# Router scores on GpSimd in two halves of four experts, with the queries' layer norms between them

## The chip, the cores and the metric

One Trainium2 chip, one of its cores. A core has a matrix engine (PE, whose weight loads are listed apart as PEld), a vector engine (DVE), a scalar engine (ACT), GpSimd (POOL) and SyncE (SP), which here only issues transfers. Each engine works through its own queue in order; semaphores tie the queues together. The metric is device time in microseconds of one execution: the median of repeated runs.

## The reference

One block of a network over 64 sequences of 32 rows with 256 features, so 2048 tokens, in float32:

```python
x = x + cross_attention(layernorm(x), ctx_512)   # 16 heads of 64, 257 context rows of 128 features per sequence
x = x + self_attention(layernorm(x))             # 4 heads of 64, rotary positions, within a sequence of 32
x = x + experts(layernorm(x))                    # 8 experts, each token goes to 2
# in experts:
scores = einsum('bsd,nd->bsn', x, Wr) + br       # [tokens, 8]: the router's scores
w = softmax(scores); idx = top_k(scores + biases_N, 2)
val = w[idx] / sum(w[idx])
y = sum over the 2 experts of val * ((silu(x @ Wl1a) * (x @ Wl1b)) @ Wl2 + biases)
```

The change touches how `scores` is computed for most tokens, and nothing else of the result.

## The kernel before

**Tiles and stages.** The tokens lie in 16 tiles of 128 rows; a tile t holds four sequences b. The main loop runs over the 64 pairs (t, b). For each it does cross-attention: scores of the next sequence (`cross_probs`, L305: four matmuls `s`, for each the negated maximum `nmx` on DVE at L319, the exponential on ACT at L320, then for two at a time a reciprocal and the scaling `pr` on DVE at L325 and L327), the transposes `tp` of the present sequence's probabilities in two groups (L338), and the mix `pa` with the context (L348). Everything else of a tile is done in small steps between these: while tile T is in its four sequences, the steps of tile T-1 ("near") and T-2 ("far") and the queries of the next pair of tiles ("ahead") are called at places given by a table, `steps` (L932), one row per sequence for an even and an odd tile, six places a row.

**The steps of a tile** (`rest`, L557) are 13 pieces between `yield`s: the value products `pov` and the cross output (1 to 3, ending in the layer norm "s"), then self-attention: transposes, qkv, the rotary products on DVE (4 to 6), the transposes `trqk`, scores and softmax, output (7 to 10, ending in the layer norm "r" into `xr`), then `route` (L475, 11 to 13): transposes `trr` of `xr`; the router's two matmuls `pr` with eight columns, the top two experts, softmax weights; and last `pk`, a matmul that ranks the tokens of each expert, from which follow `slots`, and two indirect transfers (scatters) of `xr` into the buffer `routed` in main memory. `carry` (L553) hands the running counts to the next tile with one small POOL operation.

**Queries.** `cross_queries(c)` (L250) makes the queries for tiles 2c and 2c+1: two layer norms "q", transposes `trq`, then products over several pieces. Its first piece, the norms, is called at the end of the last sequence of an odd tile.

**A layer norm** (`normed`, L173) is statistics, aggregate and adding epsilon on DVE, a power on POOL for the reciprocal root (L183), then one DVE operation (L186) that waits for it.

**Order.** PE and SP keep the order in which the program calls them. On DVE, ACT and POOL a planner sets the order when the program is built, except for instructions passed to `keep_in_program_order`. At run time each queue is fixed and in order: whatever waits at its head holds all that stands behind it.

**Buffers** that matter: PSUM banks `a` (three, used in turn by nearly all products outside the scores), `s` (three), `t` (two). `xr` has two buffers, so the writing of `xr` for tile t waits until the scatters of tile t-2 have landed.

After the last tile come the experts: six "early" blocks of 128 token rows whose experts are surely full, counted from the tiles ranked so far when the last tile begins, then "late" blocks, run over weights loaded into three lanes. They take the time from about 585 us on.

Of the kernel before, what the change touches and what calls it, by code (L numbers as in the profile page):

```python
# [9 lines left out]
FP = mybir.dt.float32  # L10
# [40 lines left out]
def block_kernel(  # L51
# [13 lines left out]
    awo: bass.AP,  # L65
    abo: bass.AP,
    freq: bass.AP,
    wr_t: bass.AP,
    br: bass.AP,
    bias_n: bass.AP,  # L70
# [96 lines left out]
    xp = pool("xp", 3)  # L167
    tb = pool("tb", 1)

    def bank(shape, name):  # L170
        return ps.tile([P] + shape, FP, tag="a", name=name)

# [77 lines left out]
    def cross_queries(c):  # L250

        xqT = wk.tile([P, 2, 2 * P], FP, tag="xqT", name=f"xqT{c}")

        xns = [normed(2 * c + j, "q", pinned=(c == 1)) for j in range(2)]
        yield
        for j in range(2):
            transposed(xqT[:, :, j * P : (j + 1) * P], xns[j], 2, f"q{2 * c + j}")


        qh = wk.tile([P, XH // 2, 2 * P], FP, tag="qh", bufs=1, name=f"qh{c}")  # L260
        q = qp.tile([P, 8, XH, SEQ], FP, tag="q", name=f"q{c}")
        queries[c] = q

        def of_heads(i):
            pq = [bank([2, 8, SEQ], f"pq{c}_{i}_{par}") for par in range(2)]
            for mm in range(2):
                m = 2 * i + mm
                for par in range(2):
                    r = par * HD
                    nc.tensor.matmul(  # L270
                        pq[par][:, mm, :, :].rearrange("p b n -> p (b n)"),
                        xwk_sb[r : r + HD, m, :],
                        qh[r : r + HD, m, :],
                        start=True,
                        stop=True,
                    )
            for par in range(2):
                dst = q[:, :, 4 * i + par : 4 * i + par + 3 : 2, :]
                dst = dst.rearrange("p b h n -> p h b n")
                if par:  # L280
                    nc.scalar.copy(dst, pq[par])
                else:
                    nc.vector.tensor_copy(dst, pq[par])

        for i in range(4):
            yield
            pq = bank([2, 2 * P], f"pqh{c}_{i}")
            for mm in range(2):
                m = 2 * i + mm
                for k in range(2):  # L290
                    nc.tensor.matmul(  # L291
                        pq[:, mm, :],
                        xwq_sb[:, k, m * P : (m + 1) * P],
                        xqT[:, k, :],
                        start=(k == 0),
                        stop=(k == 1),
                    )
            nc.scalar.mul(qh[:, 2 * i : 2 * i + 2, :], pq, QK_SCALE)
            if i:
                yield  # L300
                of_heads(i - 1)
        yield
        of_heads(3)
# [171 lines left out]
    def route(t, xr):  # L475

        nc.gpsimd.tensor_copy(xr[:, RW - 1 : RW], token[:, t : t + 1])
        xT = wk.tile([P, 2, P], FP, tag="xrT", name=f"xrT{t}")
        transposed(xT, xr, 2, f"r{t}", t < NT - 2)
        yield  # L480
        pr = bank([NE], f"pr{t}")
        for k in range(2):
            nc.tensor.matmul(pr, xT[:, k, :], wr_sb[:, k, :], start=(k == 0), stop=(k == 1))
        sc = sm.tile([P, NE], FP, tag="rsc", name=f"rsc{t}")
        nc.vector.tensor_tensor(sc, pr, br_bc, ALU.add)
        sel = sm.tile([P, NE], FP, tag="rsel", name=f"rsel{t}")
        nc.vector.tensor_tensor(sel, sc, bn_bc, ALU.add)
        top = sm.tile([P, 8], FP, tag="rtop", name=f"rtop{t}")
        nc.vector.max(top, sel)
        idx = sm.tile([P, 8], U32, tag="ridx", name=f"ridx{t}")  # L490
        nc.vector.max_index(idx, top, sel)
        idf = sm.tile([P, 2, 1], FP, tag="ridf", name=f"ridf{t}")
        nc.vector.tensor_copy(idf[:, :, 0], idx[:, 0:2])

        two = sm.tile([P, 2, NE], FP, tag="rtwo", name=f"rtwo{t}")
# [36 lines left out]
        nc.vector.tensor_tensor(at[:, 0, :], pk, region[:, 0, :], ALU.add)  # L532
        nc.vector.tensor_tensor(two, two, at.to_broadcast([P, 2, NE]), ALU.mult)
        slot = sm.tile([P, 2], FP, tag="rslot", name=f"rslot{t}")
        nc.vector.tensor_reduce(slot, two, AX.X, ALU.add)
        slots = sm.tile([P, 2], U32, tag="rslots", name=f"rslots{t}")
        nc.vector.tensor_copy(slots, slot)
        for k in range(2):
            nc.gpsimd.indirect_dma_start(  # L539
                out=routed[:, :],  # L540
                out_offset=bass.IndirectOffsetOnAxis(ap=slots[:, k : k + 1], axis=0),
                in_=xr,
                in_offset=None,
            )
        if t >= NT - 2:

            nc.gpsimd.dma_start(out=out[t * P : (t + 1) * P, :], in_=xs[t])
        if t < NT - 1:
            seen[t] = sm.tile([P, NE], FP, tag="seen", name=f"seen{t}")
            nc.vector.tensor_tensor(seen[t], pk, both, ALU.add)  # L550
            carry(t)
# [308 lines left out]
    def rotary_tables():  # L860
# [69 lines left out]


    steps = (  # L932
        ("", "far", "ahead", "near", "far", ""),
        ("near", "far", "", "near", "far", ""),
        ("ahead", "far", "ahead", "near", "far", "ahead"),
        ("near", "", "ahead", "near", "", "far"),
        ("", "far", "ahead", "near", "far", ""),
        ("near", "far", "", "near", "far", ""),
        ("ahead", "far", "ahead", "near", "far", "ahead"),
        ("", "", "near", "near", "", "far"),  # L940
    )
    last_steps = steps[4:6] + (
        ("", "", "far", "near", "", "far"),
# [1 line left out]
    )  # L945
    kvs, probs = {0: context0}, {}
    seqs = [(t, b) for t in range(NT) for b in range(4)]
    work = {"near": last_rows(), "far": iter(()), "ahead": cross_queries(0)}
    next(work["ahead"])

    diag = [const.tile([P, AH, P], FP, name=f"diag{i}") for i in range(2)]
# [85 lines left out]
    for n, (t, b) in enumerate(seqs):  # L1037
# [22 lines left out]
        def step():  # L1060
            name = next(place)
            if name:
                next(work[name], None)
# [4 lines left out]
            scores = cross_probs(t1, b1, kvs[t1][0])  # L1068
        pr, pts = probs.pop((t, b)), []
        probs_transposed(t, b, 0, pr, pts)  # L1070
        step()
        next(scores, None)
        next(scores, None)
# [15 lines left out]
        if b == 3:  # L1089
            if t < NT - 1:  # L1090
                load_last(t)
            if t % 2:
                for _ in work["ahead"]:
                    pass
                if t + 3 < NT:
                    work["ahead"] = cross_queries((t + 3) // 2)
                    next(work["ahead"])
            for _ in work["far"]:
                pass
            work["far"] = work["near"]  # L1100
            work["near"] = rest(t, cT, lastT, u_ring[t % 3])

# [144 lines left out]
```

## Time and profile before

| | us |
|---|---|
| median of 3 runs | 801.22 (800.99 to 802.54) |
| the profiled execution, its own time | 802.53 |
| its span, first to last instruction | 800.8 |
| PE busy | 771.7 (96%) |
| DVE busy | 503.1 (63%) |
| ACT busy | 365.3 (46%) |
| POOL busy | 152.4 (19%) |
| mean granted clock of PE | 0.993 |

The span falls in two parts: the 16 tiles (to about 585 us), in which all engines work, and the expert blocks, in which PE works nearly alone. In a timeline line the first number is the start in us, the second the busy time, then engine, source line, operation, what it writes and reads, sizes, the count, and in brackets the idle time before it with what ended it. In a line of a group the numbers after the bar are total busy us, mean ns of one, and idle time before, with its causes. In a table of stretches the columns are the stretch, its length, the busy time of PE, PEld, DVE, ACT and POOL, the granted clock, the share of the transfer engines and GB/s.

### The profile page before, as it was taken

To read this page: it belongs to the slowest core of one execution; us is meant where nothing else is said; L and a number is where in the kernel's file an instruction comes from. 1 tells how busy PE (TensorE), PEld (TensorE's weight loads), DVE (VectorE), ACT (ScalarE), POOL (GpSimd) and SP (SyncE) were. 2 spreads that over 40 slices of the span, in tenths; PEclk is the share of its full clock that TensorE was granted. 3 is DMA by queue.
4 is the path that set the end of the run, shared out by engine and by line. 5 is a ranking of instruction groups with operands and counts; after the bars stand their busy time and mean duration, and the time that the engine had idled before them with its cause. 6 is when DMAs were issued, how large, how long until landed. Compare 5 with 4: busy or idle time off the path is not lost. (4 is left out here: it accounts for less than half of the span.)

```text
span 800.8 us, 15293 instructions
## 1 busy us (share of the span) xinstructions
PE 771.7 (96%) x5146; PEld 604.5 (75%) x5146; DVE 503.1 (63%) x2084; ACT 365.3 (46%) x1052; POOL 152.4 (19%) x214
## 2 busy tenths in 40 slices
PE   8899999999999999999999999999999899999994
PEld 7576677677767777777767777676678799999994
DVE  4657666766686676677677766768665633554442
ACT  3564555555465555546554555555434222212220
POOL 3001011120211111111111111121124412332332
PEclk9999999999999999999999999999999999999997
DMA  9440102021120202021110202020351396458432
GB/s 309 142 111 2 67 11 68 11 89 27 53 73 18 67 11 80 11 69 50 50 60 18 68 11 67 10 78 15 119 203 34 80 398 180 54 110 251 58 45 28
DMA packets 44258, 64.17 MB, mean 80 GB/s; under 512 B 19408, under 2 KB 35152, under 8 KB 42640
## 3 DMA queue, kind: packets, MB, share of 16 engines
q1 hardware_dynamic: 37648, 54.08, 20.8%
q0 software_dynamic: 6528, 9.06, 6.2%
q8 instruction: 43, 0.70, 0.4%
q14 instruction: 39, 0.32, 0.1%
HBM read 87.54 MB, written 13.16 MB: 126 GB/s over the span
## 5 line engine op out<-in xcount | busy, mean ns | idle before, releaser
L320 ACT ACTIVATE pr<-s,nmx 128x257 f32<-128x257 f32 x256 | 122.2, 481 | 111.8 <-DVE nmx L319 100.5
L319 DVE TENSOR_REDUCE nmx<-s 128x1 f32<-128x257 f32 x256 | 105.4, 420 | 71.0 <-PE s L315 70.4
L315 PE MATMUL s<-kv,q 128*128 128x257 f32 x512 | 143.1, 388 | 1.9 <-ACT pr L320 1.9
L348 PE MATMUL pa<-pt,kv 128*128 128x512 f32 x256 | 123.2, 604 | 5.0 <-ACT ov L372 4.9
L315 PEld LDWEIGHTS s<-kv,q 128*128 128x128 f32 x512 | 89.3, 193 | 16.7 <-ACT pr L320 3.2
L338 PEld LDWEIGHTS tp<-ident,pr 128*128 128x128 f32 x512 | 61.8, 144 | 30.6 <-issue 15.7
L338 PE MATMUL tp<-ident,pr 128*128 128x128 f32 x512 | 80.5, 279 | 1.6 <-DVE pr L327 1.6
L327 DVE TENSOR_SCALAR pr<-pr,inv 128x256 f32<-128x256 f32 x256 | 79.7, 353 | 3.4
L351 ACT COPY cT<-pa 128x512 f32<-128x512 f32 x64 | 37.5, 586 | 91.4 <-PE pa L348 91.4
L342 ACT COPY pt<-tp 128x512 f32<-128x512 f32 x128 | 75.6, 591 | 4.5 <-PE tp L338 3.5
L348 PEld LDWEIGHTS pa<-pt,kv 128*128 128x128 f32 x256 | 46.1, 190 | 39.4 <-issue 26.6
L752 POOL DMA_INDIRECT out_x<-y_late,to_late x28 | 43.5, 1555 | 104.0 <-DMA out_x<-y_late,to_late 39.0
L291 PE MATMUL pqh<-xqT,xwq_sb 128*128 128x256 f32 x256 | 60.8, 381 | 0.8 <-ACT xqT L198 0.8
L381 PE MATMUL po<-xwo_sb,ov 128*128 128x256 f32 x256 | 60.6, 379 | 0.0
L381 PEld LDWEIGHTS po<-xwo_sb,ov 128*128 128x128 f32 x256 | 48.6, 190 | 6.6
L291 PEld LDWEIGHTS pqh<-xqT,xwq_sb 128*128 128x128 f32 x256 | 47.3, 190 | 7.9 <-ACT xqT L198 1.5
L320 ACT ACTIVATION_READ_ACCUMULATOR pr<-s,nmx 128x1 f32 x256 | 52.1, 203 | 0.0
L325 DVE RECIPROCAL inv<-sums 128x2 f32<-128x2 f32 x128 | 20.8, 162 | 46.7 <-ACT pr L320 45.8
L728 ACT ACTIVATE sa_late<-pa_late,lane 128x128 f32<-128x128 f32 x72 | 20.6, 369 | 63.6 <-PE pa_late L712 63.6
L555 POOL TENSOR_SCALAR carried<-seen,is_last 128x8 f32<-128x8 f32 x15 | 5.3, 353 | 218.6 <-DVE seen L550 218.6
L539 POOL DMA_INDIRECT routed<-xr,rslots x32 | 33.0, 1032 | 59.2 <-DMA routed<-xr,rslots 22.0
L396 PE MATMUL pqkv<-awqkv_sb,xaT 128*128 128x512 f32 (+1 forms) x128 | 43.9, 486 | 0.0
(275 smaller groups left out, 1270.8 us busy)
## 6 DMA issues: line engine op xcount, KB each, us to landing
lane<-in_wall SPq DMA_DIRECT2D x24, 1028.0 KB
lane<-in_wall SPq DMA_DIRECT2D x24, 640.0 KB
lane2a<-in_wall SPq DMA_DIRECT2D x10, 1028.0 KB
kv<-in_ctx_t SPq DMA_DIRECT2D x16, 514.0 KB
kv<-in_ctx_a SPq DMA_DIRECT2D x16, 512.0 KB
lane2b<-in_wall SPq DMA_DIRECT2D x10, 640.0 KB
xg_late<-routed SPq DMA_DIRECT2D x80, 32.0 KB
x<-in_x SPq DMA_DIRECT2D x16, 128.0 KB
```

The source lines that it names most:

```text
L291: nc.tensor.matmul(pq[:, mm, :], xwq_sb[:, k, m * P : (m + 1) * P], xqT[:, k, :], start=(k == 0), stop=(k == 1),)
L315: nc.tensor.matmul(s, qb[:, g * P : (g + 1) * P], kvT[:, b, :], start=True, stop=True)
L319: nc.vector.tensor_reduce(nmx, s, AX.X, ALU.max, negate=True)
L320: nc.scalar.activation(pr[:, g, :], s, AF.Exp, bias=nmx, accum_out=sums[:, g : g + 1])
L327: nc.vector.tensor_scalar(pr[:, i, :ML], pr[:, i, :ML], inv[:, i : i + 1], None, ALU.mult)
L338: nc.tensor.transpose(tp[:, g * P : (g + 1) * P], pr[:, g, j * P : (j + 1) * P], ident)
L342: nc.scalar.copy(pt, tp)
L348: nc.tensor.matmul(pa, kvA[:, b, j, :], pts[j], start=(j == 0), stop=(j == MC - 1))
L351: nc.scalar.copy(cT[:, :, b, :], pa.rearrange("p (h n) -> p h n", n=SEQ))
L381: nc.tensor.matmul(po, ov[:, m, :], xwo_sb[:, m, :], start=False, stop=(m == XH // 2 - 1))
L396: nc.tensor.matmul(pq, xaT[:, k, :], awqkv_sb[:, k, lo:hi], start=(k == 0), stop=(k == 1))
L752: nc.gpsimd.indirect_dma_start(out=out[:, :], out_offset=bass.IndirectOffsetOnAxis(ap=self.to[:, b : b + 1], axis=0), in_=y, in_offset=Non ...
```

## The change

For the tiles 0 to 12 the router's scores are computed without PE. POOL multiplies `xr` with each expert's weight row, spread over all 128 partitions, and folds the products by pairs of experts from 256 columns to 32; DVE then sums the 32 that are left, for all eight experts at once. The eight weight rows are loaded at the start into buffers that the expert blocks use later. The POOL work of a tile is in two steps, experts 0 to 3 and 4 to 7, a sequence apart in the table. Tiles 13 to 15 keep the old way, with the tile tag `xaT` for the transposed rows.

The steps of a tile are now 14, and a third stage, "late", holds a tile's last two: they are called in the first sequence of the tile after, at its first and last place, where the sum, the top two and the weights, and then `pk` and the scatters are made. `pk` thus moves from the end of a tile's fourth sequence to the end of the next tile's first one. The norms of the next queries are called at the start of an odd tile's fourth sequence instead of its end, ahead of the second half, and their first statistics are kept in program order, as are the multiplications and the sum.

```diff
+    wr_rows = []
+    for e in range(NE):
+        tag, bufs = (("y", 4), ("bxT", 2), ("wr_row", 2))[(e > 3) + (e > 5)]
+        wr_rows.append(xp.tile([P, D], FP, tag=tag, bufs=bufs, name=f"wr_row{e}"))
+        load(wr_rows[e], wr[e, :].partition_broadcast(P))
...
-        xns = [normed(2 * c + j, "q", pinned=(c == 1)) for j in range(2)]
+        xns = [normed(2 * c + j, "q", pinned=(c > 0)) for j in range(2)]
...
     def route(t, xr):
         nc.gpsimd.tensor_copy(xr[:, RW - 1 : RW], token[:, t : t + 1])
-        xT = wk.tile([P, 2, P], FP, tag="xrT", name=f"xrT{t}")
-        transposed(xT, xr, 2, f"r{t}", t < NT - 2)
-        yield
-        pr = bank([NE], f"pr{t}")
-        for k in range(2):
-            nc.tensor.matmul(pr, xT[:, k, :], wr_sb[:, k, :], start=(k == 0), stop=(k == 1))
         sc = sm.tile([P, NE], FP, tag="rsc", name=f"rsc{t}")
-        nc.vector.tensor_tensor(sc, pr, br_bc, ALU.add)
+        if t < NT - 3:
+            part = wk.tile([P, NE, SEQ], FP, tag="rpart", bufs=1, name=f"rpart{t}")
+            for e in range(0, NE, 2):
+                prod = wk.tile([P, 2, D], FP, tag="v_last", bufs=1, name=f"rprod{t}_{e}")
+                if e == NE // 2:
+                    yield
+                for i in range(2):
+                    tc.keep_in_program_order(
+                        nc.gpsimd.tensor_tensor(
+                            prod[:, i, :], xr[:, 0:D], wr_rows[e + i], ALU.mult
+                        )
+                    )
+                n = D // 2
+                while n >= SEQ:
+                    dst = prod[:, :, :n] if n > SEQ else part[:, e : e + 2, :]
+                    nc.gpsimd.tensor_tensor(dst, prod[:, :, :n], prod[:, :, n : 2 * n], ALU.add)
+                    n //= 2
+            yield
+            sums = sm.tile([P, NE], FP, tag="rsums", name=f"rsums{t}")
+            tc.keep_in_program_order(nc.vector.tensor_reduce(sums, part, AX.X, ALU.add))
+            nc.vector.tensor_tensor(sc, sums, br_bc, ALU.add)
+        else:
...
     steps = (
-        ("", "far", "ahead", "near", "far", ""),
+        ("late", "far", "ahead", "near", "far", "late"),
         ("near", "far", "", "near", "far", ""),
-        ("ahead", "far", "ahead", "near", "far", "ahead"),
-        ("near", "", "ahead", "near", "", "far"),
+        ("ahead", "far", "ahead", "near", "", "ahead"),
+        ("near", "far", "ahead", "near", "", ""),
 ...
-        ("ahead", "far", "ahead", "near", "far", "ahead"),
-        ("", "", "near", "near", "", "far"),
+        ("ahead", "far", "ahead", "near", "", "ahead"),
+        ("", "far", "near", "near", "", ""),
     )
...
         probs_transposed(t, b, 0, pr, pts)
+        if b == 3 and t % 2:
+            for _ in work["ahead"]:
+                pass
+            if t + 3 < NT:
+                work["ahead"] = cross_queries((t + 3) // 2)
+                next(work["ahead"])
         step()
...
         if b == 3:
             if t < NT - 1:
                 load_last(t)
-            if t % 2:
-                for _ in work["ahead"]:
-                    pass
-                if t + 3 < NT:
-                    work["ahead"] = cross_queries((t + 3) // 2)
-                    next(work["ahead"])
-            for _ in work["far"]:
+            for _ in work["late"]:
                 pass
+            work["late"] = work["far"]
             work["far"] = work["near"]
             work["near"] = rest(t, cT, lastT, u_ring[t % 3])
```

More of the change, by code (lines that the diff above doesn't have):

```diff
@@ L67, in block_kernel @@
     freq: bass.AP,
+    wr: bass.AP,
     wr_t: bass.AP,
@@ L477, in route @@
         nc.gpsimd.tensor_copy(xr[:, RW - 1 : RW], token[:, t : t + 1])
-        xT = wk.tile([P, 2, P], FP, tag="xrT", name=f"xrT{t}")
-        transposed(xT, xr, 2, f"r{t}", t < NT - 2)
-        yield
-        pr = bank([NE], f"pr{t}")
-        for k in range(2):
-            nc.tensor.matmul(pr, xT[:, k, :], wr_sb[:, k, :], start=(k == 0), stop=(k == 1))
-        sc = sm.tile([P, NE], FP, tag="rsc", name=f"rsc{t}")
-        nc.vector.tensor_tensor(sc, pr, br_bc, ALU.add)
+        sc = sm.tile([P, NE], FP, tag="rsc", name=f"rsc{t}")
+        if t < NT - 3:
[20 more added lines that the diff above has]
+        else:
+            xT = wk.tile([P, 2, P], FP, tag="xaT", name=f"xrT{t}")
+            transposed(xT, xr, 2, f"r{t}", t < NT - 2)
+            yield
+            pr = bank([NE], f"pr{t}")
+            for k in range(2):
+                nc.tensor.matmul(
+                    pr, xT[:, k, :], wr_sb[:, k, :], start=(k == 0), stop=(k == 1)
+                )
+            nc.vector.tensor_tensor(sc, pr, br_bc, ALU.add)
         sel = sm.tile([P, NE], FP, tag="rsel", name=f"rsel{t}")
@@ L932, in block_kernel @@
     steps = (
-        ("", "far", "ahead", "near", "far", ""),
+        ("late", "far", "ahead", "near", "far", "late"),
         ("near", "far", "", "near", "far", ""),
-        ("ahead", "far", "ahead", "near", "far", "ahead"),
-        ("near", "", "ahead", "near", "", "far"),
-        ("", "far", "ahead", "near", "far", ""),
+        ("ahead", "far", "ahead", "near", "", "ahead"),
+        ("near", "far", "ahead", "near", "", ""),
+        ("late", "far", "ahead", "near", "far", "late"),
         ("near", "far", "", "near", "far", ""),
-        ("ahead", "far", "ahead", "near", "far", "ahead"),
-        ("", "", "near", "near", "", "far"),
+        ("ahead", "far", "ahead", "near", "", "ahead"),
+        ("", "far", "near", "near", "", ""),
     )
@@ L947, in block_kernel @@
     seqs = [(t, b) for t in range(NT) for b in range(4)]
-    work = {"near": last_rows(), "far": iter(()), "ahead": cross_queries(0)}
+    work = {"near": last_rows(), "far": iter(()), "late": iter(()), "ahead": cross_queries(0)}
     next(work["ahead"])
@@ L1222 @@
         "freq": a["L0_attn_nrope_freq"],
+        "wr": a["L0_ffn_Wr"],
         "wr_t": a["L0_ffn_Wr"].T,
```

## The prediction

> **What bounds the kernel now.** I read the page's busy shares first, then stretches of 50 us, then the groups of the operations that the change removes or adds, and last the timelines around one tile boundary.
>
> ```profile
> span 800.8 us, 15293 instructions
> PE 771.7 (96%) x5146; PEld 604.5 (75%) x5146; DVE 503.1 (63%) x2084; ACT 365.3 (46%) x1052; POOL 152.4 (19%) x214
> ...
> 250.00:300.00 50.00, 49.63 (x305) 36.32 (x304) 34.22 (x144) 28.14 (x79) 8.03 (x14) 1.00 0.11 35
> ```
>
> In the cross-attention stretch PE is busy 49.63 of 50 us at full granted clock, and two tiles repeat every 72.06 us (tp of tile 6's sequence 0 starts at 232.41, of tile 8's at 304.45). So only PE work taken out shortens this stretch, and any new wait of PE lengthens it. POOL is nearly idle: 8 of 50 us.
>
> ```profile
> L356 POOL TENSOR_TENSOR xb<-x,xbo_bc 128x256 f32<-128x256 f32 x16 | 11.6, 726 | 160.9 <-issue 116.2 <-DVE x L386 28.7 <-DMA xbo_bc<-in_xbo 8.9
> ...
> L183 POOL TENSOR_TENSOR rstdq<-veq,minus_half 128x1 f32<-128x1 f32 x16 | 8.8, 552 | 19.1 <-DVE veq L181 16.6 <-DVE mvq L179 2.6
> ...
> L555 POOL TENSOR_SCALAR carried<-seen,is_last 128x8 f32<-128x8 f32 x15 | 5.3, 353 | 218.6 <-DVE seen L550 218.6
> ```
>
> These group lines price POOL: 0.727 us for a tensor operation of 256 elements, 0.55 for a norm's power, 0.315 (median) for 8 elements.
>
> PE's timeline prices what goes away, from start to next start, since matmuls overlap:
>
> ```profile
> 325.71 0.38 PE L197 MATMUL trr<-ident,xr 128*128 128x128 f32 x2
> 325.93 0.49 PE L338 MATMUL tp<-ident,pr 128*128 128x128 f32 x3
> ...
> 329.18 0.51 PE L483 MATMUL pr<-wr_sb,xrT 128*128 128x8 f32 x4
> 329.55 0.68 PE L348 MATMUL pa<-pt,kv 128*128 128x512 f32 x1
> ```
>
> The weak place is the boundary after an odd tile (tile 7 to 8), on DVE and on PE's weight loads:
>
> ```profile
> 303.97 0.17 DVE L325 RECIPROCAL inv<-sums 128x2 f32<-128x2 f32 x1 [0.43 <-ACT pr L320]
> 304.17 0.61 DVE L327 TENSOR_SCALAR pr<-pr,inv 128x256 f32<-128x256 f32 x2
> ...
> 305.50 0.28 DVE L411 TENSOR_TENSOR qkv<-qkv,x2s 128x128 f32<-128x128 f32 x1
> ...
> 305.99 0.41 DVE L319 TENSOR_REDUCE nmx<-s 128x1 f32<-128x257 f32 x1
> ```
> ```profile
> 304.45 0.59 PEld L338 LDWEIGHTS tp<-ident,pr 128*128 128x128 f32 x4
> ...
> 305.84 0.46 PEld L197 LDWEIGHTS trqk<-ident,qkv 128*128 128x128 f32 x4
> ```
> ```profile
> 309.27 0.85 PEld L364 LDWEIGHTS pov<-cT,xwv_sb 128*64 128x64 f32 x16 [0.20 <-ACT xqT L198]
> ```
>
> The last scaled probabilities end at 304.78; the transposes that read them start at 304.45 and take 0.59 us where four elsewhere take 0.47. The rotary result ends at 305.78 and trqk loads at 305.84. DVE is packed from 304.17 to 306.8. At this boundary PE has no slack on DVE; in the middle of a tile the same transposes come 1.5 to 4.7 us after their data.
>
> **The change part by part.**
>
> PE loses, in 13 tiles, two transposes (0.22 us) and the router's matmuls (0.37): 0.59 x 13 = 7.7 us. ACT's xrT copy (0.37) and the wait for xr go too; both lay beside PE work.
>
> The rank matmul pk moves from the end of sequence 3 to the end of the next tile's sequence 0. It costs PE 0.14 us (341.20 to tp at 341.34). Where it goes away, nothing is won: the transposes behind it wait for DVE until 304.78 either way. Where it lands it costs 0.14 x 13 = 1.8 us. So PE gains 7.7 - 1.8 = 5.9 us, if nothing waits.
>
> POOL gains per tile 8 multiplications and 4 additions at 0.727, and 4 additions each of 128 and 64 elements, which no row has. Bounds are 0.315 and 0.727; on a straight line between those two rows they are 0.51 and 0.41, which I take. With 0.06 between dependent operations (the gap in front of axb) a half is 6.6 us, bounds 5.6 (no gaps) and 7.8. Two halves are 13.2 us a tile: POOL has the room. The question is its order.
>
> In even tiles nothing stands between the halves. xr is ready at 324.97; from 325.05 both halves run to 338.2, perhaps 340.5 with the collisions below. The new reduction of the sums stands on DVE just before the next tile's first nmx, at about 341.9 in this frame. It is covered by more than 1 us. Cover gone, each us costs 7 us over seven tiles.
>
> In the odd tiles 3 to 11 the queries' norms stand between. DVE's order in sequence 3 becomes: q copy, statistics, nmx, xn (waits for POOL), statistics, nmx, nmx, second xn (waits for POOL), and only then the scaling L327. Before, these norms were in sequence 2, where DVE idles. The stretch that receives them:
>
> ```profile
> 297.69 0.68 DVE L283 COPY q<-pq 128x512 f32<-128x512 f32 x1
> 298.59 0.86 DVE L319 TENSOR_REDUCE nmx<-s 128x1 f32<-128x257 f32 x2 [0.21 <-PE s L315]
> 299.90 0.43 DVE L319 TENSOR_REDUCE nmx<-s 128x1 f32<-128x257 f32 x1 [0.45 <-PE s L315]
> ```
>
> I lay the new order on it, everything 0.59 earlier. Half one starts at 290.45 (xr straight after the tile's own norm, as in even tiles) and ends near 297.1, in time. q copy ends 297.6; statistics, aggregate and epsilon (0.4, 0.2, 0.15) reach 298.4; the power ends 299.0; xn to 299.4; second statistics to 299.8; two nmx and the small steps to 300.7; second power to 301.3. POOL runs in order, so half two starts at 301.3 and ends at 307.9. DVE itself, 0.7 us late from the waits, would reach the reduction at 306.5. So it waits for POOL, takes 0.35, and nmx comes at 308.3. Without the wait it would be 305.99 - 0.59 = 305.4: 2.9 us late. Behind it queue ACT's exponentials and then the xqT copies, for which pov at 309.27 already waits. ACT's router exponential now stands before the second exponential there and adds 0.3. PE loses 2.9 + 0.3 = 3.2 us, five times: 16 us.
>
> Bounds: with the shortest half (5.6) POOL is done when DVE arrives and the loss is DVE's lateness alone: 306.5 + 0.35 - 305.4 + 0.3 = 1.75, or 8.8 in all. If DVE is not late either, 0.35 + 0.3 = 0.65 stays, 3.3 in all. With half two at 7.8 and every collision against POOL (eight at 0.35, 2.8 us) POOL ends at 311.9 and the loss is 7.2, or 36.
>
> The boundary after tile 13 has no norms between: only the 0.3.
>
> DVE and POOL collide. One row shows it:
>
> ```profile
> 71.63 1.09 DVE L327 TENSOR_SCALAR pr<-pr,inv 128x256 f32<-128x256 f32 x2
> ...
> 71.85 0.72 POOL L467 TENSOR_TENSOR axb<-x,abo_bc 128x256 f32<-128x256 f32 x1 [6.28 <-issue]
> ```
>
> Two scalings take 0.62 us elsewhere, 1.09 here: +0.47. Within POOL's 13.2 us of a tile fall two to four such pairs. In sequences 2 and 3 they have 1.5 us and more of slack: nothing. After odd tiles the pair at 304.17 is hit, but what is lost there lies inside the wait for POOL already counted. POOL's own delay no row shows; bounds 0 and 0.35 (one scaling) each; I take 0, since POOL's 0.725 in that row is its usual time.
>
> The Trainium skill (SBUF — State Buffer, "Who interferes with whom") says more: a DVE instruction with two SBUF inputs also blocks against a GpSimd instruction that reads SBUF, for the whole instruction. Here the rows disagree for small ones (router steps at 609.74 and 609.95, inside a power of POOL, took 174 and 166 ns against medians of 167 and 146), and no run here shows it for large ones. By that rule the seven rotary and p_last operations from 302.3 to 305.8 would hold POOL up by about 7 x 0.28 = 2 us per boundary, and the sum would be near 822; by the row alone it is the one below.
>
> Eight loads of 128 KB go ahead of the second tile's context on SP, at 0.47 us each or more: 4 to 8 us later. That context is moving by 28 to 32 us and first read at 49.8 (scores of tile 1): covered. The scatters move a sequence later; POOL's second one then ends about 9 us into sequence 1, where xb is due at 8.8: covered, at most 0.5 us for the norm behind it, whose transposes have 5 us. The gathers before the expert blocks have about 10 us between sequence 1 of the last tile and their first use.
>
> Sum: -5.9 + 16.0 + 0.3 = +10.4 us. The profiled execution took 802.53 us (span 800.8 and 1.7 around), 1.3 above the median of 801.22. Against the median: 811.6 us.
>
> **The rivals.**
>
> Faster: POOL finishes before DVE asks. That needs a second power before about 299.5 and a half below 6 us, so that the reduction never waits. For it speaks POOL's emptiness; against it the two round trips DVE to POOL in sequence 3. Worth -5.9 + 0.3 = -5.6: 795.6 us. With 0.65 per boundary it is 798.9. The gain is eaten up, and the change turns slower, from 1.1 us per boundary.
>
> Much slower: collisions stretch POOL in every tile. Then the even boundaries lose their 1.2 us of cover too. For it speaks +0.47 in the one row; against it that POOL lost nothing there. -5.6 + 36, and 1 us in seven even tiles, give 839 at worst, some 820 with half of both.
>
> The change does not shorten PE: excluded in the order of instructions, where trr and pr are gone from 13 tiles, but at a DVE-bound boundary the 0.59 us could be lost again: 801.2 + 1.8 = 803.
>
> **How the numbers follow.** POOL late after the odd tiles, as summed: 0.57, its own range 804 to 816. Much slower: 0.15. PE gain lost: 0.06. Faster: 0.17. No change: 0.05. A measurement tells about 0.2% (1.6 us). Slower is 0.57 + 0.15 + 0.06 = 0.78. The range 799 to 822 leaves out most of the faster case and the far end of the worst.
>
> **What would show it.** No trr and pr of the first 13 tiles on PE; POOL near 25 of 50 us. DVE idle before the new reduction, ended by POOL, 1 us or more, in tiles 4, 6, 8, 10, 12 alone. PE idle at the pov of those tiles, ended by ACT xqT. A period of two tiles near 74 us instead of 72.06. L327 with a maximum over 0.6 us many times. I am wrong if that reduction does not wait, if POOL's small additions are far from 0.51 and 0.41, or if DVE's order in sequence 3 runs ahead of my times.

## The result, and the profile after

| | before | after |
|---|---|---|
| median of 5 runs beside each other | 802.54 us (800.99 to 806.51) | 825.86 us (823.64 to 829.57) |
| the profiled execution, its own time | 802.53 | 824.45 |
| its span | 800.8 | 822.2 |
| until the first transposes `tp` of tile 1 | 55.0 | 53.1 |
| from there to `tp` of the last tile's fourth sequence ("the tiles") | 522.0 | 542.1 |
| from there to the end ("the rest") | 223.8 | 227.1 |

The ratio is 1.0287, 95% interval 1.0246 to 1.0328. The kernel became slower, as forecast, but by 23 us and not by 10, and outside the range of 799 to 822. The two us at the start are none of the change's: that part took 52.9 to 55.4 us in the runs below, in no order with what was edited there.

The head of the page after, and the stretch that was shown of before:

```profile
span 822.2 us, 15385 instructions
PE 775.2 (94%) x5068; PEld 604.2 (73%) x5068; DVE 532.0 (65%) x2097; ACT 362.7 (44%) x1039; POOL 305.8 (37%) x474
...
250.00:300.00 50.00, 49.65 (x302) 36.69 (x301) 33.64 (x129) 26.60 (x76) 24.66 (x41) 1.00 0.13 41
```

POOL went from 8 to 24.66 of 50 us. PE has 78 instructions fewer and is busy longer. The groups of the new POOL work, forms kept apart:

```profile
L497 POOL TENSOR_TENSOR rprod<-xr,wr_row 128x256 f32<-128x256 f32 x104 | 74.9, 741 | 7.9 <-DVE xr L194 4.7 <-PE pqh L298 0.5
...
L504 POOL TENSOR_TENSOR rprod<-rprod 128x256 f32<-128x256 f32 x52 | 38.0, 732 | 4.1
...
L504 POOL TENSOR_TENSOR rprod<-rprod 128x128 f32<-128x128 f32 x52 | 23.9, 459 | 4.1
L504 POOL TENSOR_TENSOR rpart<-rprod 128x64 f32<-128x64 f32 x52 | 16.8, 323 | 4.1
```

A half of four experts takes 6.4 to 6.5 us. The time is lost in one place. Taking as the mark of each sequence the start of the weight load (PEld) of its first `tp`, an odd tile's fourth sequence and the next tile's first together took 14.99 us before and take 20.31 after (mean of the five boundaries behind tiles 3 to 11); I call these two "the boundary pair". That is 5 x 5.32 = 26.6 us. All other sequences together are 6.5 us shorter. What ends PE's idle time there, in the tables of waits of before and of after:

```profile
PE tp L338 <- DVE pr L327: 1.6, 1, 1.6
```
```profile
PE tp L345 <- DVE pr L334: 18.0, 10, 2.9
```

The columns after the colon are us in all, times, the longest. PE waits for the scaling of the probabilities. DVE's timeline at the boundary of tiles 7 and 8 after:

```profile
305.15 0.41 DVE L194 TENSOR_SCALAR xnq<-x,mvq,rstdq 128x256 f32<-128x256 f32 x1 [0.33 <-POOL rstdq L191]
...
307.35 0.80 DVE L194 TENSOR_SCALAR xnq<-x,mvq,rstdq 128x256 f32<-128x256 f32 x1 [0.33 <-POOL rstdq L191]
308.07 1.62 DVE L334 TENSOR_SCALAR pr<-pr,inv 128x256 f32<-128x256 f32 x2
...
312.12 1.43 DVE L334 TENSOR_SCALAR pr<-pr,inv 128x256 f32<-128x256 f32 x2
...
313.55 0.41 DVE L414 TENSOR_TENSOR x1s<-qkv,sin 128x128 f32<-128x128 f32 x1
...
314.60 0.41 DVE L508 TENSOR_REDUCE rsums<-rpart 128x8 f32<-128x256 f32 x1
```

Half two runs on POOL from 307.28 to 313.81. Within it the second xn takes 0.80 instead of 0.41, a pair of scalings 1.62 and 1.43 instead of 0.61. The new reduction at 314.60 has no wait in front of it: when DVE comes to it, POOL has been done for 0.8 us. The same place on PE:

```profile
309.93 0.38 PE L345 MATMUL tp<-ident,pr 128*128 128x128 f32 x2
313.16 0.98 PE L345 MATMUL tp<-ident,pr 128*128 128x128 f32 x2 [2.85 <-DVE pr L334]
313.94 1.92 PE L322 MATMUL s<-kv,q 128*128 128x257 f32 x4
315.65 1.06 PE L205 MATMUL trqk<-ident,qkv 128*128 128x128 f32 x4
```

After the wait the four `s` take 1.92 us where elsewhere four take 1.03, and `trqk` 1.06 where 0.60 is usual: the granted clock has dropped. The two stretches:

```profile
309.50:313.13 3.63, 0.81 (x4) 0.28 (x2) 3.13 (x9) 1.04 (x3) 3.24 (x7) 1.00 0.51 149
313.13:316.50 3.37, 3.19 (x10) 2.50 (x11) 2.98 (x14) 1.15 (x3) 0.60 (x2) 0.52 0.61 231
```

So three things were open: whether the longer scalings (collisions with POOL) make the wait, or the norms moved into the fourth sequence, or the stage late; what the clock's drop costs; and why the rest takes 3.3 us more. The scaling's durations (min/median/max) before and after:

```profile
L327 DVE TENSOR_SCALAR pr<-pr,inv x256: 334/350/834, 19.4 to 577.1; 128x256 f32<-128x256 f32 x128
```
```profile
L334 DVE TENSOR_SCALAR pr<-pr,inv x256: 342/354/909, 19.0 to 595.2; 128x256 f32<-128x256 f32 x128
```

Above 400 ns lie 3 of 256 before, 71 after.

### The profile page after: what moved, and what is told of

Read it like the earlier page. It is cut to its first block, busy times and chain, and to the rows that moved or that the text cites. A ratio compares the mean times of both kernels' runs of the same rounds, so it can differ in the third digit from the quotient of the medians.

```text
span 822.2 us, 15385 instructions
## 1 busy us (share of the span) xinstructions
PE 775.2 (94%) x5068; PEld 604.2 (73%) x5068; DVE 532.0 (65%) x2097; ACT 362.7 (44%) x1039; POOL 305.8 (37%) x474
## 2 busy tenths in 40 slices
DMA packets 45985, 68.62 MB, mean 83 GB/s; under 512 B 19600, under 2 KB 36368, under 8 KB 44112
## 5 line engine op out<-in xcount | busy, mean ns | idle before, releaser
L322 PE MATMUL s<-kv,q 128*128 128x257 f32 x512 | 146.9, 395 | 2.8 <-ACT pr L327 1.9
L322 PEld LDWEIGHTS s<-kv,q 128*128 128x128 f32 x512 | 91.3, 197 | 18.4 <-ACT pr L327 6.9
L345 PE MATMUL tp<-ident,pr 128*128 128x128 f32 x512 | 86.4, 284 | 19.2 <-DVE pr L334 18.0
L345 PEld LDWEIGHTS tp<-ident,pr 128*128 128x128 f32 x512 | 63.9, 146 | 52.8 <-ACT cT L358 18.0
L334 DVE TENSOR_SCALAR pr<-pr,inv 128x256 f32<-128x256 f32 x256 | 100.2, 429 | 3.6
L349 ACT COPY pt<-tp 128x512 f32<-128x512 f32 x128 | 75.1, 587 | 15.2 <-PE tp L345 13.8
L497 POOL TENSOR_TENSOR rprod<-xr,wr_row 128x256 f32<-128x256 f32 x104 | 74.9, 741 | 7.9 <-DVE xr L194 4.7
L504 POOL TENSOR_TENSOR rprod<-rprod 128x256 f32<-128x256 f32 x104 | 61.9, 595 | 8.2
```

Of the source, the lines that this page charges most:

```text
L322: nc.tensor.matmul(s, qb[:, g * P : (g + 1) * P], kvT[:, b, :], start=True, stop=True)
L334: nc.vector.tensor_scalar(pr[:, i, :ML], pr[:, i, :ML], inv[:, i : i + 1], None, ALU.mult)
L345: nc.tensor.transpose(tp[:, g * P : (g + 1) * P], pr[:, g, j * P : (j + 1) * P], ident)
L349: nc.scalar.copy(pt, tp)
L497: nc.gpsimd.tensor_tensor(prod[:, i, :], xr[:, 0:D], wr_rows[e + i], ALU.mult)
L504: nc.gpsimd.tensor_tensor(dst, prod[:, :, :n], prod[:, :, n : 2 * n], ALU.add)
```

## The experiments

All times are medians; the kernel before, run beside them, had 802.4 to 803.9. Pairs, tiles, rests and waits are those of one profiled execution. In the code cuts, comments are mine, and `...` marks what is left out.

**The norms back at their old place.** The changed kernel with

```diff
-        xns = [normed(2 * c + j, "q", pinned=(c > 0)) for j in range(2)]
+        xns = [normed(2 * c + j, "q", pinned=(c == 1)) for j in range(2)]
...
-        if b == 3 and t % 2:      # ahead of the first step
+        if t % 2:                 # under "if b == 3", at the end, as before
             for _ in work["ahead"]:
```

> The changed kernel, but the queries' norms are called at the end of an odd tile's fourth sequence again and are not pinned after the second pair, so that both halves of POOL's work follow each other in odd tiles as in even ones. Half two then ends before the scaling at the boundary. Theory A (half two lies on the boundary after odd tiles, DVE and POOL hold each other up there, PE waits some 3 us and its clock then drops): the excess of about 5.8 us at each of five boundaries goes, 825.9 - 29 = about 797 us, range 794 to 803; the wait of PE's tp for the scaling, 18.0 us in the changed kernel, falls below 4. Rival R2 (POOL's products slow DVE wherever they lie): stays above 815. Rival R3 (the stage late, with pk and the scatters in the first sequence, is what costs): stays above 815. Rival R1 (the norms' round trips in the fourth sequence by themselves) also gives about 797 here; the run with the scores on PE tells it from A.

853.59 us, the slowest of all: a miss for theory A, and above the 815 of the rivals R2 and R3, but not for their reasons. On DVE the planner had put the reduction ahead of the second pair of scalings:

```profile
311.76 0.40 DVE L194 TENSOR_SCALAR xnq<-x,mvq,rstdq 128x256 f32<-128x256 f32 x1
320.92 0.42 DVE L508 TENSOR_REDUCE rsums<-rpart 128x8 f32<-128x256 f32 x1 [8.76 <-POOL rpart L504]
321.26 0.15 DVE L332 RECIPROCAL inv<-sums 128x2 f32<-128x2 f32 x1
```

The wait that the prediction had put into the changed kernel stands here, five times, 43.8 us in all. The run says nothing of the collisions at the boundary, since half two ends some 10 us before it; it needed the reduction out of the way first (below).

**The scores on PE, everything else as changed.**

```diff
-        if t < NT - 3:            # products and folds on POOL
...
+        xT = wk.tile([P, 2, P], FP, tag="xaT", name=f"xrT{t}")   # all tiles: trr, pr
...
+        nc.vector.tensor_copy(sums, pr)
+        yield
```

> The changed kernel's order of steps, with the queries' norms pinned in the fourth sequence, the stage late and the eight loads of weight rows, but the scores of all tiles are made on PE (transposes, two matmuls, one copy of 8 columns on DVE) and POOL makes no products. Theory A and rival R2: without POOL's work nothing collides; 7.7 us of PE work are back on top of the 797 that the changed kernel would have without its boundaries, so 802 to 808. Rival R1 (the norms' round trips in the fourth sequence cost by themselves): above 818, and PE waits for the scaling at the boundaries after odd tiles for 2 us or more. Rival R3: above 818, too, but without that wait.

813.70 us, between the theories; ratio 1.0120 (1.0078 to 1.0163). The boundary pair takes 16.57 us: 1.6 of the 5.3 come without any POOL work. The tiles take 529.2, the rest 229.4.

**The stage late alone**: the last run with the norms at their old place.

> The changed order with the scores on PE and without products, but with the queries' norms at their old place, so that the stage late is all that is left of the change. With the norms in the fourth sequence the two sequences around the boundary took 16.58 us and the whole 813.7. If the norms' two round trips to POOL make the 1 us that PE waits there: 15.0 to 15.8 us, the whole 807 to 811. If the stage late alone makes it: 16.4 or more, and 812 to 815.

806.54 us, pair 15.72, tiles 524.2. So at the boundary the stage late costs 0.73 and the norms 0.85 us.

**The products alone, in the old order.** The kernel before with the loads of the weight rows, the tag `xaT`, and

```diff
         nc.gpsimd.tensor_copy(xr[:, RW - 1 : RW], token[:, t : t + 1])
+        if t < NT - 3:            # all four pairs of products and folds, result unused
+            ...
```

> The kernel before, with the same POOL products and folds added for tiles 0 to 12 as soon as xr is ready, into a buffer that nobody reads; the scores come from PE as before. So no step of the old order moves, and only POOL's load is new. Theory A: the products end before the boundary, collisions in the middle of a sequence are covered, 802 to 806. Rival R2 (collisions cost wherever they lie): 815 or more. If DVE's extra time over 352 ns in the scaling is as large here (20 us in the changed kernel) and the time does not move, it is the place that decides.

825.49 us, a miss for theory A (802 to 806) and as much as the changed kernel, but lost elsewhere: the pair takes 15.91 (+0.92), the even tiles' fourth sequences +1.5, the odd tiles' third +0.8. The waits of PE:

```profile
PE pqkv L403 <- DVE q L290: 7.2, 6, 1.4
...
PE pa L355 <- DVE q L290: 3.2, 5, 0.7
```

In the old order the router's small steps stand on DVE just before a copy q whose buffer PE needs next; collisions ahead of it come through: in tile 6's fourth sequence `xr<-rex,rinv` (128x8), the last of the weights, takes 0.70 us instead of 0.23 and `rboth<-rtwo` (128x8) 0.64, and PE then waits 1.17 us for q. So small steps collide too. In the changed order, where those steps lie a sequence later, the same places lose nothing. This speaks for the place and not the load; the runs with one half each, below, show it.

**Products unused in the changed order: both halves, half two, half one.** The run with the scores on PE, plus POOL's products at their changed places:

```diff
         nc.gpsimd.tensor_copy(xr[:, RW - 1 : RW], token[:, t : t + 1])
+        # products and folds of experts 0 to 3 (half one)
         xT = wk.tile([P, 2, P], FP, tag="xaT", name=f"xrT{t}")
         transposed(xT, xr, 2, f"r{t}", t < NT - 2)
         yield
+        # products and folds of experts 4 to 7 (half two)
```

> The run with the changed order and the scores on PE, and in addition POOL's products and folds at the places that they have in the changed kernel, into a buffer that nobody reads. Nothing waits for POOL's result. The two sequences around an odd tile's end (its fourth and the next tile's first) took 14.99 us before, 20.31 in the changed kernel, 16.58 with the scores on PE. Theory C (POOL's running slows the instructions of DVE that lie beside it, and DVE has no slack there): these two take 19.5 to 21 us again, and the whole 828 to 836, 3.7 us at five boundaries more than the 813.7 with the scores on PE. Rival D (waiting for the data, the reduction behind half two and what hangs on it): 16.6 to 17.5 us, the whole 814 to 820.

> As the last, but only the products of experts 4 to 7 (half two) are made, unused; half one is left out, so POOL does half the work. Theory C, with half two as the part that lies on the boundary: the two sequences around the boundary take 19 to 20.5 us, the whole 826 to 833. If half one, in the middle of the sequences before, were the cause: 16.6 to 17.5 us and 814 to 820.

> The changed order with the scores on PE and, unused, only the products of experts 0 to 3 (half one); half two is left out. The counterpart of the run with half two alone, which gave 832.0. Theory C (what lies beside DVE's scaling at the boundary costs, the rest is covered): the two sequences around the boundary take 16.6 to 17.5 us, the whole 814 to 820, near the 813.7 without any products. If POOL's load as such costs: about 823 or more.

| POOL's products | us | boundary pair | tiles |
|---|---|---|---|
| none | 813.70 | 16.57 | 529.2 |
| half one | 813.08 | 16.45 | 529.7 |
| half two | 832.04 | 21.09 | 552.8 |
| both | 833.92 | 20.78 | 552.8 |

Nothing waits for these products, and yet the pair is as long as in the changed kernel. Half two alone makes it, at the pair even more than expected; half one is free. (The profiled executions with half two and with both were 5.1 and 3.1 us longer than their medians.) PE's wait without products, with half one, with half two, with both:

```profile
PE tp L345 <- DVE pr L334: 6.4, 7, 1.6
```
```profile
PE tp L345 <- DVE pr L334: 6.7, 8, 1.6
```
```profile
PE tp L345 <- DVE pr L334: 18.2, 8, 3.0
```
```profile
PE tp L345 <- DVE pr L334: 19.5, 10, 3.0
```

Theory C holds: POOL's running beside DVE at the boundary is enough. Another way for the products to cost would be POOL's queue, in which the norms' powers could stand behind them. It is not that: DVE's waits for the powers do not grow (queries' norms 6.3 us in all without products, 5.7 with both; norms "s" 12.9 and 11.0).

PE's busy time splits what the products cost at the boundary (means of the five pairs; idle is the length less PE's busy time):

| POOL's products | PE idle, us | PE busy, us | granted clock |
|---|---|---|---|
| none | 1.15 | 15.42 | 1.00 |
| both | 3.35 | 17.43 | 0.84 to 0.92 |
| the changed kernel | 3.35 | 16.96 | 0.84 to 0.92 |

Of the 4.2 us, 2.2 are waiting and 2.0 are PE working longer on the same work at a lower clock. In the trace's record of the clock, three of the five pairs with both halves have one stretch of 3.41 us at half clock and take 20.04 to 20.50 us; the other two have 6.83 us of it and take 21.58 and 21.67, at the same idle time. So each such stretch costs 1.1 to 1.7 us.

**The scaling on ACT.** The changed kernel, in the first sequence of tiles 4 to 12:

```diff
+                    if t in ON_ACT and b == 0:
+                        nc.scalar.mul(pr[:, i, :ML], pr[:, i, :ML], inv[:, i : i + 1])
+                        continue
```

> The changed kernel, but the four scalings of the probabilities of the first sequence of tiles 4, 6, 8, 10 and 12, which end last at the boundary, are made by ACT. ACT reads the same data and does not show longer instructions beside POOL in the changed kernel. Theory C: the 2.4 us that the two pairs and the xn before them lose on DVE go in part, and DVE has 1.2 us less to do: the two sequences take 16.5 to 18 us instead of 20.31, the whole 808 to 816. If DVE's lateness isn't what PE waits for, or ACT is as late: 822 or more.

818.24 us, pair 18.88: the right direction, less than expected, a miss of the range. Two lines of DVE at the same boundary say why:

```profile
309.16 0.82 DVE L423 TENSOR_TENSOR qkv<-qkv,x1s 128x128 f32<-128x128 f32 x1
...
311.72 0.42 DVE L512 TENSOR_REDUCE rsums<-rpart 128x8 f32<-128x256 f32 x1 [1.54 <-POOL rpart L508]
```

Rotary steps now take the collisions (0.82 instead of 0.28), and behind them the predicted wait of the reduction for POOL comes up, 1.54 us. Behind the reduction the chain of the prediction follows: PE waits 8.9 us in all at `s` for the exponentials (1.9 in the changed kernel) and 2.1 at `pov` for xqT (none there). The two causes stand one behind the other; who removes the first meets the second. PE's idle time in the pair barely falls, from 3.35 to 3.12 us. What is won is mostly the clock: the longest wait there is 1.41 us, and the pairs' clock is 1.00.

**The norms at their old place and the sum later.** The first run, with the reduction called in the middle of the sequence after odd tiles (a place may now name two stages):

```diff
-        ("late", "far", "ahead", "near", "far", "late"),
+        ("", "far", "late ahead", "near", "far", "late"),
```

> The run with the norms at their old place, but after odd tiles the first piece of the stage late (the sum of POOL's products, the top two, the weights) is called in the middle of the next sequence instead of its start. There the reduction stood ahead of the scaling on DVE and waited 8.76 us for POOL. Theory C with D for that run: the reduction no longer waits; POOL's half two still lies on the boundary, but without norms in front of the scaling DVE has slack, as in the run with the unused products in the old order (15.92 us for the two sequences). So 16 to 17 us, the whole 801 to 811. If half two on the boundary is enough by itself: 19 us or more, the whole 818 or more.

802.29 us, ratio 0.9998 (0.9975 to 1.0021); pair 15.84, tiles 518.7, 3.3 us less than before. Over the whole kernel most collisions are still there, 63 scalings above 400 ns:

```profile
L334 DVE TENSOR_SCALAR pr<-pr,inv x256: 335/354/894, 19.2 to 572.1; 128x256 f32<-128x256 f32 x128
```
```profile
296.43 1.02 DVE L334 TENSOR_SCALAR pr<-pr,inv 128x256 f32<-128x256 f32 x2
...
300.17 1.03 DVE L334 TENSOR_SCALAR pr<-pr,inv 128x256 f32<-128x256 f32 x2
```
```profile
PE tp L345 <- DVE pr L334: 2.3, 3, 1.6
```

The first pair ends 2.5 us before its transposes (`tp` loads from 300.00) and only the second is felt. In the changed kernel the same pair, behind the norms, ends 0.2 us after the loads begin (309.69 and 309.50): there is no slack left. But the run changes a second thing: half two, no longer behind the second norm, runs from 5.46 us before the boundary's mark to 1.05 after it, instead of from 2.22 before to 4.3 after, and the two pairs of scalings lose 0.8 us there and not 1.8. What the slack and what the earlier half two are worth by themselves, no run separates.

**PE kept busy in the wait.** The changed kernel with ten matmuls of `ident` by itself ahead of the first `tp` of tiles 4 to 12.

> The changed kernel, with ten matmuls of the identity by itself into the buffer of the transposes, ahead of the first transposes of tiles 4, 6, 8, 10 and 12, where PE waits for DVE; the transposes overwrite it. They take about 0.24 us each, so they fill most of the wait of 2.9 us and delay nothing. If the drop of the granted clock to 0.52 after the wait comes from PE's idling, it goes, and with it 1.5 us at each of five boundaries: about 818. If the drop has another cause, the time stays at 826, or grows by up to 2 us where the filling is longer than the wait.

829.80 us. The mean granted clock rose from 0.981 to 0.993 and `s` took 1.03 again, so PE's idling does bring the drop. The time did not fall, against the 818 expected, but the run is not clean: the planner moved the router's steps ahead of the first `nmx` on DVE, and PE waited for what follows:

```profile
PE s L324 <- ACT pr L329: 9.8, 8, 1.6
```

So this run doesn't price the drop. At the boundary of tiles 7 and 8 of the changed kernel the longer `s` and `trqk` alone are 0.9 + 0.5 = 1.4 us, in line with the 1.1 to 1.7 us above.

**The rest: early counts.** All runs with the stage late moved more bytes. Before, after, and the products alone in the old order, from the pages' lines on transfers:

```profile
DMA packets 44258, 64.17 MB, mean 80 GB/s; under 512 B 19408, under 2 KB 35152, under 8 KB 42640
```
```profile
DMA packets 45985, 68.62 MB, mean 83 GB/s; under 512 B 19600, under 2 KB 36368, under 8 KB 44112
```
```profile
DMA packets 45412, 65.24 MB, mean 79 GB/s; under 512 B 19536, under 2 KB 36304, under 8 KB 43792
```

1.05 MB are the eight weight rows. The other 3.4 MB are two experts' weights (1028 and 640 KB each): a lane's weights are loaded only where a block's expert differs from the lane's last one. The early blocks are counted from the tiles ranked when the last tile begins, `counted("early", max(seen))`; with the stage late that is one tile less, so the blocks fall to other experts. Three runs on it: the kernel before with `max(seen) - 1`; the last version with tile 12 done the old way in time; and the last version with `early_blocks()` called in the last tile's second sequence.

> The kernel before, with one edit: the early blocks are counted from one ranked tile less. In the changed kernel the stage late ranks tile 12 a sequence later, so that when the last tile begins only tiles 0 to 11 are ranked; after the last tile's fourth sequence the changed kernel and all runs with the stage late take 2.6 to 5.6 us longer, with the transfer engines at 374 GB/s in a stretch of 4 us where the kernel before moves 33. Theory T (other counts give other experts to the early blocks, so weights are loaded that were reused before): the tiles take their 577 us as before, the rest 226 to 230 instead of 223.8, the whole 804.5 to 809. If the counts don't matter: 802.

> The run with the norms at their old place and the sum later (802.3; tiles 572.0 us, rest 229.4), but tile 12 goes the old way too, with the scores on PE and its ranking done before the last tile begins. Theory T: the rest falls back to 223.5 to 225 us, the tiles take 572 to 573.5 (two transposes and the router's matmuls are back once), the whole 796 to 799. If the rest of 229.4 has another cause, it stays: 802 to 804.

> The run with the norms at their old place and the sum later (802.3; tiles 572.0 us, rest 229.4), with all of tiles 0 to 12 on POOL, but the early blocks are counted a sequence later, in the last tile's second sequence, when tile 12 is ranked. Theory T (the counts of one tile less give other experts to the early blocks, whose weights must be loaded): the rest falls to 224 to 226 us, the tiles stay at 572 to 573.5, the whole 796.5 to 800 beside a kernel before of 802.4 to 803.9. If the rest has another cause than the counts: the rest stays at 228 or more, the whole 801 to 804.

| | us | tiles | rest | MB |
|---|---|---|---|---|
| before, counts of one tile less | 803.51 | 521.8 | 226.8 | 67.59 |
| sum later | 802.29 | 518.7 | 229.4 | 68.62 |
| sum later, tile 12 on PE | 800.33 | 519.4 | 226.9 | 65.21 |
| sum later, counted a sequence later | 799.31 | 517.8 | 225.4 | 65.21 |

The bytes follow the counts exactly, and with them the waits of the early blocks' first product for a lane's weights (3.4 us in the changed kernel, 2.6 us with the sum later, none in the last two). The rest follows only in part: the first of these had 3 us more in its profile and no more in its median (804.5 to 809 was expected), and tile 12 on PE kept 3.1, with other waits, and missed its 796 to 799. And the products alone in the old order had a rest of 229.1 without extra weights: there 15.2 us follow PE's last instruction, 10.3 before, where the last scatters came late. Nor do the loads alone set the rest: the stage late alone and half one alone moved the same 68.6 MB, waited 2.8 and 2.4 us for the lanes' weights, and had rests of 224.9 and 225.7.

A second wait tells the runs apart: that of the late blocks' first transposes, `pxT_late`, for their gathered rows, `xg_late`. It is 3.2 us with the sum later (rest 229.4) and at most 3.8 with the scores on PE (229.4), each followed by a stretch at half clock, 6.83 us with the sum later, which is worth up to 3.4. It is 1.3 in the two runs with the short rests, at most 0.3 before and 0.5 in the last two, and none of these has such a stretch behind it. No run tests what makes this wait. And executions of the kernel before scatter over 7 us, so that 2 or 3 us between single profiles decide little. So the extra loads and their cause are shown, their price only roughly: 229.4 to 225.4 and 802.3 to 799.3 between two kernels that differ in the moment of the count alone. The last version is 0.5% faster than the kernel before: ratio 0.9950 (0.9928 to 0.9973).

## Why the prediction was right and wrong

**Direction and place: right.** The five boundaries behind tiles 3 to 11 were named, and 26.6 us are lost there; the first sequences of the last two tiles lose 1.4 and 2.6 more, that of tile 2 1.1. The boundaries after even tiles were covered, as said: 0.89 us longer than before, less than the 1.15 without any POOL work.

**The step that failed** is "what is lost there lies inside the wait for POOL already counted". The reduction does not wait in the changed kernel. DVE itself is late: the second xn loses 0.4, the two pairs of scalings 1.0 and 0.8 us, 2.2 together, in a chain where every one is at once PE's wait. They were costed at nothing because a later wait was to hide them; but the scaling stands ahead of the reduction on DVE, and PE waits for the scaling, so a wait at the reduction can't hide it. A second cost was missing: the sum has no term for PE's clock, which fell to half after that wait. Predicted were 3.2 us per boundary, found 5.3. By the runs: 0.7 from the stage late (predicted 0.3 and pk's 0.14), 0.9 from the norms (I had 0.7 us for DVE), 4.2 from POOL's two halves beside it, less 0.5 for PE's work that is gone (20.78 to 20.31). The 4.2 are 2.2 of PE's waiting, as much as the collisions, and 2.0 of its work at the lower clock. PE's idle time per boundary grew by 3.0 us over before (0.37 to 3.35), close to the 3.2 forecast, but from another wait: that agreement is luck.

**The wait of the reduction** was right as a mechanism and wrong for this kernel. It came up in two of the runs, 8.76 and 1.54 us, where DVE reached it sooner. Of the signs named, POOL's 25 of 50 us and the many long scalings came; DVE's wait at the reduction and PE's at `pov` did not, and the period of two tiles was 75.3 to 75.8 us, not 74.

**POOL's half**: predicted 6.6, measured 6.4 to 6.5; the folds of 128 and 64 elements took 0.459 and 0.323 instead of 0.51 and 0.41.

**PE's gain**: against the run with both halves unused, where PE still makes the scores, an even tile's second to fourth sequences are 0.6 us shorter, an odd tile's first three 0.5 and its fourth 0.4; 0.59 a tile was predicted. pk does gain where it leaves (with the stage late alone, the fourth sequences took in the router's matmuls, 0.37 by the prediction, and were still 0.06 shorter: about 0.4) and costs more where it lands; the stage late as a whole costs the tiles 2.2 us, against 1.8 predicted for pk.

**The rivals.** "Much slower", 820 to 839 us, has the time but not the mechanism: POOL did not stretch. Half one, clear of most of DVE's large steps, took 6.42 us, half two among them 6.53.

**Two SBUF inputs.** The Trainium skill (SBUF — State Buffer, "Who interferes with whom") says that a vector instruction with two SBUF inputs contends with a GpSimd instruction that reads SBUF. The runs agree: steps with two inputs took 0.41 at 313.55 after, and 0.82 with the scaling on ACT, instead of 0.28; but not every one is longer (`qkv<-qkv,cos` beside POOL 0.275, elsewhere 0.282). The prediction doubted it for small steps; 0.64 for `rboth<-rtwo` in the old order, against its median of 0.146, shows that they are hit too. Its use of the rule was wrong in one more point: it made POOL pay 2 us; here DVE paid and POOL 0.1. And the sentence doesn't cover the largest losses, of the scaling and of xn, which read one tensor and one or two numbers per row.

**The rest** was costed at nothing and is 3.3 us longer in the profile: the scatters' delay was looked at, but not the count that reads the ranks. The eight loads at the start were hidden, as said.

## What to carry to other kernels

A collision costs what the colliding instruction's slack doesn't hold: the same longer scalings cost next to nothing where they ended 2.5 us early, and took part in a loss of 4 us a boundary where they had no slack. And a wait of PE can cost more than its length: here one of about 3 us was followed by 2 us lost at half clock. Before hiding one loss inside another wait, check that the wait stands behind it on the same queue and not after the point where the next engine is released. When a stage is moved later, look for whoever reads its running result at a fixed moment: a count taken one tile short loaded 3.4 MB more.

## What the hardware showed

A wait of PE of 2.85 us was followed by 3.41 us at half the clock (0.52 over the stretch shown), and so at four of the five boundaries; at the fifth by 6.83 us. At the same places waits of 0.78 us, with the scores on PE, and of 1.41, with the scaling on ACT, brought no drop. The length of the wait alone doesn't decide: a wait of 1.6 us some 24 us after the start was followed by 3.41 us at half clock in the kernel before, and not with the scores on PE. The Trainium skill (TensorE: Matmul & The Clock Gate, Part 1) has the clock halved after an idle window of about 3.4 us; here a stretch of 3.63 us in which PE was busy for 0.81 was enough.

DVE's longer steps beside POOL's products are those that read and write SBUF alone. In the changed kernel the scaling took 0.55 us (median of 78 that lay by more than half beside a product or fold) instead of 0.35, the queries' xn 0.815 instead of 0.414, the rotary step x1s 0.409 instead of 0.284. What reads PSUM kept its time: the maximum 0.424 instead of 0.419, the copy q 0.690 instead of 0.686.
